# A build-time planner that knows TensorE's tile widths, matmuls over rows of zeros, and copies for whichever engine is free

## The chip, the cores and the metric

The kernel runs on one core of a Trainium2 chip. The metric is the device time of one execution in microseconds (us), the median of several runs. Profiles are of one execution each; their span, from the first to the last instruction, is some 50 us shorter than the device time.

## The reference

16 images of 336x336 pixels become 441 tokens each, 128 text tokens follow, so there are 16 sequences of T = 569 tokens of D = 256. Two layers work on them, all in f32:

```
h = concat(tokens(x), txt)
# layer 0
h = h + window_attention(layernorm(h))      # windows of 64, 8 heads, shifted
h = h + experts(layernorm(h))               # 8 experts, the 2 best of each token
# layer 1
h = h + phasor_attention(layernorm(h))
h = h + lstm_block(layernorm(h))

def phasor_attention(x):                    # a linear attention with a running state
    key_phase   = tanh(gelu(x @ Wk1 + bk1) @ Wk2 + bk2) * freq * pi
    query_phase = tanh(gelu(x @ Wq1 + bq1) @ Wq2 + bq2) * freq * pi
    V = x @ Wv + bv
    memory = cumsum(exp(i key_phase) * V, over tokens)
    r = real(sum(memory * exp(-i query_phase))) / sqrt(position * 64)
    return x + (layernorm(r) * ln_w + ln_b) @ Wo + bo

def lstm_block(x):                          # 569 steps, one after another
    gates = x @ W_ih.T + b + h @ W_hh.T     # i, f, g, o
    c = sigmoid(f) * c + sigmoid(i) * tanh(g);  h = sigmoid(o) * tanh(c)
    # then a sum over earlier and later tokens with a gate from h @ W_lin
```

## The kernel before

All work is cut into small generators. Each `yield` names an engine and a planned duration (`yield "ACT", 0.58`), and the instructions that follow it are that piece of work. A planner, `Order` (its `run`), holds many such streams at once. It keeps the time at which each engine is planned to be free, always takes the piece that can start first (ties go to the lower rank, then to the earlier stream), and emits its instructions. All of this happens when the program is built: on the chip, each engine executes a fixed list in that order, and only semaphores hold it back.

`first = Order()` plans the first part: `features` and `projections` (image features), `tokens` (attention of the tokenizer, two streams), `norms`, `windows` (window attention, four streams), `routing`. `plan = Order()` plans the rest: `experts`, and then the flow. Engines are TensorE (PE), VectorE (DVE), ScalarE (ACT) and GpSimd (POOL); a `+` after a name (`DVE+`) stands for the use of a resource that DVE and POOL share.

In the flow, four background streams work on units of two pairs of sequences and one column chunk of 128 rows: `fronts` (two slots, function `front`: combining the experts' outputs, norm, keys, queries and values) and `backs` (two slots, function `back`: reading from the state, norm, output projection, norm, and the LSTM's input projection, split into three bf16 pieces by L1495, L1497, `rest_of_pieces`, and written to XPD). `add_to_state` (ds, L1348) adds each chunk to the running state S. A batch is four units of one chunk, and two batches make one block of 64 time steps for the LSTM; `stats` and `norm` are shared helpers.

The stream `steps()` is the LSTM chain. It is special: its operations have a fixed table of planned durations (`STEP`), and the planner takes background pieces only into the gaps that its function `limits` leaves. The rule is this line, with `spare` the overrun that is allowed:

```
spare = 0.15 if engine == "PE" else 0.0 if "+" in engine else 0.1
...
if start + taken > end + spare and not (start > s.ready + 8.0 and start < end - 0.5):
    continue
```

One LSTM step is 16 hidden matmuls 16 columns wide (L1614, planned as `hidden`), then the next step's two `input` matmuls (L1584, L1585), gates on ACT (L1628, L1631), products and cell on DVE (L1634, L1640), two 32x32 transposes (L1646, L1649), tanh (L1652), and X, the new hidden state (L1654). `all_sums` handles the sums after every 16 steps.

PE's array can be used in narrower tiles. Matmuls with 64 output columns go side by side (tokens L548, L576; windows L681, L696, L736; state reads L1431), 32 wide ones in the router (L781) and in `hidden`; ds takes 64 rows of keys at a time, and the biases of V and of the output projection are added by matmuls of three rows (three bf16 pieces of the bias, times ones: L1283, L1451). The planner before adds one constant, `SWITCH = 0.09`, whenever a piece marked `"small"` follows one that is not, or the reverse.

Of the kernel before, what the change touches and what calls it, by code (L numbers as in the profile page):

```python
# [17 lines left out]
D = 256  # L18
# [85 lines left out]

ENGINES = {
# [5 lines left out]

HOP = 0.06
OVERLAP = {"PE": 0.0, "DVE": 0.08, "ACT": 0.1, "POOL": 0.03}
DRAIN = 0.17
SWITCH = 0.09
# [26 lines left out]
class Order:  # L142
    def __init__(self):
        self.free = dict.fromkeys(("PE", "DVE", "ACT", "POOL", "+"), 0.0)
        self.events, self.ends = {}, dict.fromkeys(STEP, 0.0)
        self.now, self.table, self.small = 0.0, None, False
        self.forks, self.held, self.freed = [], set(), {}
# [63 lines left out]
    def run(self, streams, until=None):  # L211
        streams = [s if isinstance(s, Stream) else Stream(s) for s in streams]
        for s in streams:
            if s.head is None and not s.over:
                self.advance(s)
        while self.forks or not all(s.over for s in (until or streams)):
            for s in self.forks:
                self.advance(s)
            streams = [s for s in streams if not s.over] + self.forks
            self.forks = []  # L220
            for s in streams:
                self.settle(s)
            if all(s.over for s in (until or streams)):
                continue
            chain = [s for s in streams if s.chain and not self.blocked(s)]
            limit, best = {}, None
            if chain:
                limit = self.limits(chain[0])
                engine, us = STEP[chain[0].head][:2]
                best = (limit[uses(engine)[0]], -1, -1, chain[0], engine, us)  # L230
            for n, s in enumerate(streams):
                if s.chain or self.blocked(s):
                    continue
                engine, us = s.head[:2]
                kind = s.head[2] if len(s.head) > 2 else None
                if engine == "PE":
                    us += SWITCH * ((kind == "small") != self.small)
                elif kind not in (None, self.table):
                    us += 1.3
                start = max([s.ready] + [self.free[e] for e in uses(engine)])  # L240
                end = min(limit.get(e, 1e9) for e in uses(engine))
                spare = 0.15 if engine == "PE" else 0.0 if "+" in engine else 0.1
                taken = us - OVERLAP[engine.strip("+")]
                if start + taken > end + spare and not (start > s.ready + 8.0 and start < end - 0.5):
                    continue
                if best is None or (start, s.rank, n) < best[:3]:
                    best = (start, s.rank, n, s, engine, us)
            assert best is not None, "all streams wait"
            start, _, _, s, engine, us = best
            if s.chain:  # L250
                for e in uses(engine):
                    self.free[e] = start + us
                self.ends[s.head] = start + STEP[s.head][2]
                s.ready = start + us
                if engine == "PE":
                    self.small = s.head == "hidden"
            else:
                for e in uses(engine):
                    self.free[e] = start + (us if e == "+" else us - OVERLAP[e])
                if engine == "PE":  # L260
                    self.small = len(s.head) > 2
                elif len(s.head) > 2:
                    self.table = s.head[2]
                s.ready = start + us
            was = engine
            self.advance(s)
            if not s.chain and not s.over and s.head[0].strip("+") != was.strip("+"):
                s.ready += HOP + DRAIN * (was == "PE")


@with_exitstack
def kernel(ctx: ExitStack, tc: tile.TileContext, a: dict, out: bass.AP):
# [264 lines left out]
    def tokens(slot):  # L537

        last = NIMG - 384
        for n in range(slot, 7 * NP, 2):  # L540
# [4 lines left out]
            for m in range(2):  # L545
                yield "PE", 0.8, "small"
                for s in range(2):
                    nc.tensor.matmul(  # L548
                        sc[64 * s : 64 * s + 64, :NIMG], QT[s][:, m, 64 * c : 64 * c + 64],
                        fTs[2 * p + s][:, m, :], start=(m == 0), stop=(m == 1),  # L550
                    )
# [20 lines left out]
            for t in range(4):  # L572
                m = min(128, NIMG - 128 * t)
                yield "PE", 0.5, "small"
# [66 lines left out]
    def windows(slot):  # L641

        kb, vb = KB[slot], VB[slot]
        for n in range(slot, NC * NP, WINDOWS):
# [33 lines left out]
            for m in range(2):  # L678
                yield "PE", 0.46, "small"
# [12 lines left out]
            for w in range(2):  # L692
                for k in range(2):
                    yield "PE", 0.26, "small"
# [36 lines left out]
            for m in range(2):  # L731
                for w in range(2):
                    yield "PE", 0.16, "small"
# [22 lines left out]
    def routing():  # L756

        for p, lo, hi in PARTS:
            u, n = f"{p}_{lo}", hi - lo
            pr = wk.tile([128, n, E], F32, name=f"pr{u}", tag="pr", bufs=1)  # L760
            for g0 in range(lo, hi, 4):
# [16 lines left out]
                for k in range(2):  # L778
                    yield "PE", 0.42, "small"
# [172 lines left out]
    one3 = ls.tile([3, 128], BF16, name="one3")  # L952
    nc.vector.memset(one3, 1.0)

    bias3 = {n: ls.tile([3, 2, D], BF16, name=f"{n}3") for n in ("l1_bv", "l1_bo")}
# [217 lines left out]


# [27 lines left out]
    def norm(src, mv, rstd, name, slot):  # L1202
        xn = wk.tile([128, 2, D], F32, name=name, tag=f"xn{slot}")
        for c in range(src.shape[1]):
            yield ("DVE", 0.54) if name[0] == "r" else ("DVE+", 0.42)
            nc.vector.tensor_scalar(
                xn[:, c, :], src[:, c, :], mv[:, c, 0:1], rstd[:, c : c + 1],
                ALU.subtract, ALU.mult,
            )
        return xn  # L1210
# [12 lines left out]
    def front(p, c, n, at, slot):  # L1223
# [34 lines left out]
        yield "ACT", 0.55  # L1258
        nc.scalar.copy(xT, tr)
# [22 lines left out]
        yield "PE", 0.32  # L1282
# [8 lines left out]
        yield "ACT", 0.58  # L1291
        nc.scalar.copy(V[:, both, :], v)
        z = bank(f"z{u}", slot).rearrange("p (k n) -> p k n", k=2)
        y = wk.tile([128, 2, 256], F32, name=f"fy{u}", tag=f"fy{slot}")
# [37 lines left out]

    def add_to_state(p, c, u, slot, S2, kT, V, at):

        for s in range(2):
            half = slice(64 * s, 64 * s + 64)
# [6 lines left out]
            for j in range(2):  # L1343
                yield ("PE", 0.43) if c == 8 else ("PE", 0.53, "small")
                lhs, rhs = (
                    (kT[:, j, :], own[:, j, :]) if c == 8 else (kT[half, j, :], V[half, at + j, :])
                )
                nc.tensor.matmul(ds[:, j, :], lhs, rhs, start=True, stop=True)  # L1348
# [31 lines left out]
    def back(p, c, batch, at, slot, late=False):  # L1380
# [24 lines left out]
        if not late:  # L1405
# [3 lines left out]
            kT = wk.tile([128, 2, 128], F32, name=f"kT{u}", tag=f"kT{slot}")  # L1409
            yield "ACT", 0.38  # L1410
            nc.scalar.copy(kT, sc[:, :, 1, :])
# [12 lines left out]
        for j in range(2):  # L1424
            yield "PE", 256 * COLUMN
            nc.tensor.matmul(r[:, j, :], w[:, j, :], V[:, at + j, :], start=True, stop=not reads)
            if reads:
                yield "PE", 0.55, "small"
# [11 lines left out]
        for k in range(2):  # L1440
            yield "DVE", 0.34 if c8 else 0.54
            src, to = tr[:, k, :], nT[:, k, :]
            if c8:
                src = src.rearrange("p (b x) -> p b x", x=64)[:, :, r0 : r0 + 32]
                to = to.rearrange("p (b x) -> p b x", x=32)
            nc.vector.tensor_scalar(
                to, src, col("ln_w", k), col("ln_b", k), ALU.mult, ALU.add
            )
        po = bank(f"po{u}", slot)[:, : D * n].rearrange("p (k n) -> p k n", k=n)
        yield "PE", 0.32 if n == 2 else 0.2  # L1450
# [25 lines left out]
        yield "ACT", 0.3 * n  # L1476
        nc.scalar.copy(xT, tr)  # L1477
        to = XPD[block].rearrange("(i q b) t d -> i q b t d", i=3, q=4)
        for i in range(2 * n):
# [14 lines left out]
            yield "ACT", 0.58  # L1494
            nc.scalar.copy(pieces[:, 0, :], mm)  # L1495
# [248 lines left out]
    with tc.manual_schedule(engines=ENGINES):  # L1744
# [5 lines left out]
        wk = bg.enter_context(tc.tile_pool(name="pha", bufs=1))  # L1750
        chain, rest = Stream(steps(), True), Stream(all_sums())
# [165 lines left out]
```

## Time and profile before

| | before |
|---|---|
| time, median of 3 | 3776.37 us (3773.66 to 3778.86) |
| span of the profiled execution | 3726.4 us, mean granted clock of PE 0.965 |
| busy: PE, DVE, ACT, POOL | 87%, 57%, 38%, 25% |
| hidden matmuls, L1614 | 9088 records, the costliest group, 612.8 us |
| chain that ended last | PE 33%, DVE 12%, ACT 5% of the span |

The page divides the span into 40 slices of 93 us, and the digits there are busy tenths. A group's line gives the source line, the engine, the operation, the tile written and the tiles read, the shape, the count, busy time and mean duration, and at its end how long the engine had been idle ahead of it and what ended that idle time. In a line of stretches, each engine has its busy time and its number of instructions (x), then follow the clock that PE was granted, and the share and rate of the DMA. A matmul in f32 appears as two records of one instruction each, which start apart by their streaming time and overlap in duration, so starts tell more than durations.

### The profile page before, as it was taken

What the parts mean: (1) busy time and instruction counts of PE and PEld (TensorE: products, weight loads), DVE (VectorE), ACT (ScalarE), POOL (GpSimd) and SP (SyncE); (2) the same over time, 40 slices, a digit from 0 to 9 for tenths busy, and PEclk for the clock granted to TensorE, in tenths of its full rate; (3) what the DMA queues carried; (4) which work ended last, traced back from release to release, by engine and by line L of the source; (5) the groups of instructions that cost most, each with busy time, mean ns of one, the idle gap of its engine ahead of it and who ended that gap; (6) DMA issues with size and microseconds to landing.
All of it is one profiled execution on the core that took longest, in us unless ns stands there. A gap on an engine that the chain in (4) does not pass through costs nothing.

```text
span 3726.4 us, 67881 instructions
## 1 busy us (share of the span) xinstructions
PE 3249.1 (87%) x24854; PEld 2095.9 (56%) x24854; DVE 2121.5 (57%) x6447; ACT 1398.8 (38%) x4098; POOL 944.0 (25%) x1627
## 2 busy tenths in 40 slices
PE   6989998899839999996899999999999999998663
PEld 3656565555538888885556555555555555544331
DVE  4666666665631111113476677777777777676444
ACT  3444454444312222223444444444444444333220
POOL 1244344443520000004433322222222222121000
PEclk9999999999969999998999999999999999999997
DMA  4111112100166666653324333333333333333214
GB/s 159 53 57 61 62 67 75 41 28 22 46 216 221 228 231 225 231 175 101 98 79 120 104 84 94 99 91 97 97 94 103 100 87 91 91 106 117 86 38 101
DMA packets 276950, 398.13 MB, mean 107 GB/s; under 512 B 29008, under 2 KB 234056, under 8 KB 263560
## 3 DMA queue, kind: packets, MB, share of 16 engines
q1 hardware_dynamic: 254712, 347.44, 29.9%
q0 software_dynamic: 13824, 37.77, 3.4%
q10 hardware_dynamic: 8080, 8.57, 0.7%
q8 instruction: 196, 3.21, 0.4%
q14 instruction: 138, 1.13, 0.1%
HBM read 256.60 MB, written 136.97 MB: 106 GB/s over the span
## 4 chain that ended last, share of the span: by engine, by line
PE 33%; DVE 12%; ACT 5%; issue 2%; POOL 1%; DMA 1%; SPq 0%; ACTq 0%; DVEq 0%; POOLq 0%
PE g L1614 13%; PE xm_False L1486 4%; DVE ab L1634 2%; PE g L1584 2%; PE v L1287 2%; DVE act L1640 2%; ACT th L1652 2%; DVE cT L1646 2%; ACT act L1628 2%; PE z L1298 2%; PE eq L1267 2%; PE ek L1267 2%; DVE X L1654 1%; PE ds_False L1348 1%; PE po_False L1455 1%
## 5 line engine op out<-in xcount | busy, mean ns | idle before, releaser
L1614 PE MATMUL g<-W_hh,X 128*16 128x256 f32 x9088 | 612.8, 388 | 169.6 <-DVE X L1654 165.6
L1614 PEld LDWEIGHTS g<-W_hh,X 128*16 128x16 f32 x9088 | 208.9, 96 | 464.0 <-DVE X L1654 332.9
L1628 ACT ACTIVATE act<-g 128x192 f32<-128x192 f32 x568 | 187.9, 331 | 593.8 <-PE g L1614 592.2
L1634 DVE SCALAR_TENSOR_TENSOR ab<-act 128x128 f32<-128x128 f32 x568 | 172.2, 303 | 388.0 <-ACT act L1628 380.9
L1239 POOL DMA_INDIRECT yg<-YS,yat x144 | 142.9, 992 | 660.1 <-DMA YS<-ys 622.8
L1153 ACT ACTIVATE hT<-hp,w 128x256 f32<-128x256 f32 x316 | 132.5, 472 | 456.2 <-PE hp L1146 293.3
L1160 PE MATMUL y<-w,hT 128*128 128x256 f32 x1264 | 289.9, 382 | 6.3 <-ACT hT L1153 2.5
L1364 POOL TENSOR_TENSOR xp_False<-left_False,xp_False 128x256 bf16<-128x256 f32 x272 | 182.4, 691 | 425.9 <-ACT xp_False L1361 408.5
L1146 PE MATMUL hp<-xt,w 128*128 128x256 f32 x1264 | 285.8, 379 | 0.0
L1486 PE MATMUL xm_False<-W_ih,dxT_False 128*128 128x256 f32 x1088 | 272.4, 384 | 9.0 <-ACT dxT_False L1477 7.5
L1652 ACT ACTIVATE th<-cT 128x32 f32<-128x32 f32 x569 | 130.0, 228 | 359.9 <-DVE cT L1646 353.9
L1160 PEld LDWEIGHTS y<-w,hT 128*128 128x128 f32 x1264 | 236.7, 190 | 46.8 <-ACT hT L1153 16.1
L1166 DVE TENSOR_TENSOR ys<-y,w 128x512 f32<-128x512 f32 x79 | 54.6, 691 | 357.8 <-PE y L1160 357.8
L1146 PEld LDWEIGHTS hp<-xt,w 128*128 128x128 f32 x1264 | 239.0, 190 | 33.9
L1486 PEld LDWEIGHTS xm_False<-W_ih,dxT_False 128*128 128x128 f32 x1088 | 196.4, 191 | 39.7 <-ACT dxT_False L1477 10.5
L1654 DVE SCALAR_TENSOR_TENSOR X<-toT,th 128x32 f32<-128x32 f32 x569 | 116.3, 204 | 116.9 <-ACT th L1652 116.8
L1584 PEld LDWEIGHTS <-pick 128*128 128x128 bf16 x569 | 54.6, 96 | 214.5 <-issue 212.1
L663 PE MATMUL wqk<-wxT,wqkv 128*128 128x128 f32 x1152 | 164.2, 285 | 10.7 <-ACT wxT L657 10.5
L663 PEld LDWEIGHTS wqk<-wxT,wqkv 128*128 128x128 f32 x1152 | 144.6, 193 | 41.4 <-ACT wxT L657 19.9
L872 POOL DMA_INDIRECT XS<-XN,at x144 | 149.3, 1037 | 58.8 <-DVE at L865 29.4
L1584 PE MATMUL g<-xp,pick 128*128 128x256 bf16 x569 | 161.4, 284 | 1.8 <-DMA xp<-XPD 1.8
L1585 PE MATMUL g<-xp,pick 76*128 76x256 bf16 x569 | 157.9, 278 | 3.6 <-DMA xp<-XPD 3.6
(337 smaller groups left out, 6416.7 us busy)
## 6 DMA issues: line engine op xcount, KB each, us to landing
w<-in_wpack SPq DMA_DIRECT2D x79, 1154.0 KB
XPD<-xp_False SPq DMA_DIRECT2D x408, 128.0 KB
xp<-XPD SPq DMA_DIRECT2D x71, 512.0 KB
taps<-in_taps SPq DMA_DIRECT2D x16, 1764.0 KB
xs<-XS SPq DMA_DIRECT2D x79, 256.0 KB
YS<-ys SPq DMA_DIRECT2D x79, 256.0 KB
xp<-XPD SPq DMA_DIRECT2D x71, 256.0 KB
HD<-h SPq DMA_DIRECT2D x72, 128.0 KB
```

The lines of the kernel that those rows point to most:

```text
L663: nc.tensor.matmul(qk[:, j, m, :], wqkv[:, k, D * j + 128 * m : D * j + 128 * m + 128], xT[:, k, :], start=(k == 0), stop=(k == 1),)
L1146: nc.tensor.matmul(hp[:, i, :], w1[:, k, hc * 128 : (hc + 1) * 128], xT[:, k, :], start=(k == 0), stop=(k == 1),)
L1160: nc.tensor.matmul(y[:, i, :], hT[:, hc, 128 * i : 128 * i + 128], w2[:, hc, :], start=(hc == 0), stop=(hc == 3),)
L1364: nc.gpsimd.tensor_tensor(pieces[:, 2, h], left[:, h], pieces[:, 1, h], ALU.subtract)
L1486: nc.tensor.matmul(mm[:, 256 * part : 256 * part + 256], xT[:, k, j * 128 : (j + 1) * 128], Wih[:, k, at_ : at_ + 256], start=(k == 0), st ...
L1584: nc.tensor.matmul(g, pick[:, 0, :], xp[:, 0, t, :], start=True, stop=False)
L1585: nc.tensor.matmul(g, pick[:76, 1, :], xp[:76, 1, t, :], start=False, stop=(k, t) == (0, 0))
L1614: nc.tensor.matmul(g[32 * q : 32 * q + NB, :D], before[:, kk, :], Whh[:, kk, q * D : (q + 1) * D], start=False, stop=(kk == 1),)
L1628: nc.scalar.activation(act[:, :192], g[:, :192], AF.Tanh, scale=0.5)
L1634: nc.vector.scalar_tensor_tensor(ab, act[:, :128].rearrange("p (g x) -> p g x", g=2), 1.0, act[:, 128:].rearrange("p (g x) -> p g x", g=2) ...
L1652: nc.scalar.activation(th, cT[:, :, :NB], AF.Tanh, scale=0.5)
L1654: nc.vector.scalar_tensor_tensor(X[:, :, t, :], toT[:, :, :NB], 1.0, th, ALU.add, ALU.mult)
```

## The change

The change has four parts.

The planner's costs. `SWITCH` is replaced by costs to enter and to leave a tile width (`TO_TILES`, `FROM_TILES`), per width, and pieces are marked "64" or "32" instead of "small", with new durations. A piece of another width than PE has now is ranked as if it started 0.3 us (`SAME_TILES`) later. The overrun into the chain's gaps falls from 0.15 to 0.1 for PE and from 0.1 to 0 for DVE and ACT.

Free choice. A piece can be `"DVE/ACT"` with one duration for each; the planner takes the engine where it starts first, and the helper `copy` emits the instruction for that engine. Copies of fxT, V, dxT, kT, the first bf16 piece, and the scale-and-shift operations of the norm of r and of nT are such pieces. For this the norm of r is computed as scale and bias, which needs one small operation (`less`).

Full tiles. The bias matmuls run over 128 rows, of which all but three are zero in the bias. For ds, the keys of the two halves lie in two persistent tiles for each slot, each with zeros in the other half's rows, and the matmul takes all 128 rows of V.

Memory. `fy` shares the buffers of `xn`, as the persistent key tiles need room.

```diff
-SWITCH = 0.09
+TO_TILES = {None: 0.0, "32": 0.11, "64": 0.15}
+FROM_TILES = {None: 0.0, "32": 0.1, "64": 0.19}
+SAME_TILES = 0.3
...
-                if engine == "PE":
-                    us += SWITCH * ((kind == "small") != self.small)
...
-                spare = 0.15 if engine == "PE" else 0.0 if "+" in engine else 0.1
...
+                either = s.head[0] == "DVE/ACT"
+                kind = s.head[2] if len(s.head) > 2 and not either else None
+                for engine, us in zip(("DVE", "ACT"), s.head[1:]) if either else [s.head[:2]]:
+                    other = kind != self.tiles if engine == "PE" else kind not in (None, self.table)
+                    if other:
+                        us += 1.3 if engine != "PE" else FROM_TILES[self.tiles] + TO_TILES[kind]
+                    start = max([s.ready] + [self.free[e] for e in uses(engine)])
+                    key = start + (SAME_TILES if other and engine == "PE" else 0.0)
...
+                    spare = 0.1 if engine == "PE" else 0.0
...
-                yield "PE", 0.8, "small"
+                yield "PE", 0.76, "64"
...
-    one3 = ls.tile([3, 128], BF16, name="one3")
+    one3 = ls.tile([128, 128], BF16, name="one3")
...
-    bias3 = {n: ls.tile([3, 2, D], BF16, name=f"{n}3") for n in ("l1_bv", "l1_bo")}
+    bias3 = {n: ls.tile([128, 2, D], BF16, name=f"{n}3") for n in ("l1_bv", "l1_bo")}
...
+    def copy(to, src, scale=None, bias=None):
+        if plan.chosen == "DVE":
...
+        if name[0] == "r":
+            less = wk.tile([128, 2], F32, name=name + "_less", tag=f"less{slot}", bufs=1)
+            yield "DVE", 0.17
+            nc.vector.scalar_tensor_tensor(
+                less, mv[:, :, 0], -1.0, rstd, ALU.mult, ALU.mult
+            )
+            for c in range(src.shape[1]):
+                yield "DVE/ACT", 0.54, 0.46
+                copy(xn[:, c, :], src[:, c, :], rstd[:, c : c + 1], less[:, c : c + 1])
+            return xn
...
-        yield "PE", 0.32
+        yield "PE", 0.22
         nc.tensor.matmul(v, one3, bias3["l1_bv"], start=True, stop=False)
...
-        yield "ACT", 0.58
-        nc.scalar.copy(V[:, both, :], v)
+        yield "DVE/ACT", 0.69, 0.58
+        copy(V[:, both, :], v)
...
-                yield ("PE", 0.43) if c == 8 else ("PE", 0.53, "small")
-                lhs, rhs = (
-                    (kT[:, j, :], own[:, j, :]) if c == 8 else (kT[half, j, :], V[half, at + j, :])
-                )
-                nc.tensor.matmul(ds[:, j, :], lhs, rhs, start=True, stop=True)
+                yield "PE", 256 * COLUMN
+                rhs = own[:, j, :] if c == 8 else V[:, at + j, :]
+                nc.tensor.matmul(
+                    ds[:, j, :], kT[0 if c == 8 else s][:, j, :], rhs, start=True, stop=True
+                )
...
-            kT = wk.tile([128, 2, 128], F32, name=f"kT{u}", tag=f"kT{slot}")
-            yield "ACT", 0.38
-            nc.scalar.copy(kT, sc[:, :, 1, :])
+            kT = keys_of[slot]
...
+            for s in range(0 if c8 else 2):
+                half, other = (slice(64 * i, 64 * i + 64) for i in (s, 1 - s))
...
+                yield "DVE/ACT", 0.41, 0.38
+                copy(kT[s][half], sc[half, :, 1, :])
...
-            yield "ACT", 0.58
-            nc.scalar.copy(pieces[:, 0, :], mm)
+            yield "DVE/ACT", 0.69, 0.58
+            copy(pieces[:, 0, :], mm)
```

## The prediction

> **What bounds the kernel now.** I read the page first for the stages, then busy time by stretch, then the chain's own lines, then TensorE (PE) in order of time.
>
> ```profile
> PE   6989998899839999996899999999999999998663
> PEclk9999999999969999998999999999999999999997
> ```
>
> Four stages stand here: the first part (0 to 1040 us), the experts (1090 to 1700), the flow with the LSTM chain (1705 to about 3430), and the chain alone. The clock hardly ever dips, so it explains none of them.
>
> ```profile
> core 0: us, PE busy (x) PEld busy (x) DVE busy (x) ACT busy (x) POOL busy (x), PEclk, DMA share, GB/s
> 50.00:950.00 900.00, 818.64 (x6632) 522.63 (x6630) 586.55 (x1499) 415.55 (x1111) 358.93 (x631) 0.99 0.15 54
> 1705.00:1984.00 279.00, 245.61 (x1470) 169.62 (x1470) 156.66 (x459) 127.67 (x305) 122.66 (x190) 0.95 0.35 99
> 2000.00:3300.00 1300.00, 1212.18 (x10490) 681.68 (x10489) 943.28 (x3217) 570.10 (x1825) 341.06 (x582) 0.98 0.34 94
> ```
>
> PE is busy 91%, 88% and 93% of these stretches; no other engine passes 73%. ACT is at 44% in the flow where DVE is at 73%. Then the LSTM's last line, L1654 (one X per step), in the same kind of view:
>
> ```profile
> 2000.00:3300.00 1300.00, 84.82 (x411) 0.98 0.34 94
> 3430.00:3680.00 250.00, 15.72 (x82) 0.99 0.19 65
> ```
>
> A step takes 1300/411 = 3.16 us beside background work and 250/82 = 3.05 us over the whole last stretch; from X to X its typical value there is 2.92 and its mean 2.94. So the chain is the clock of the flow, and the background costs each step 0.22 us. From hop to hop (mean of the crowded steps less that of the free ones) 0.11 us of it is hidden matmuls that wait for PE, 0.03 slower hidden matmuls, 0.02 and 0.03 waits for DVE and ACT, and the rest DVE operations stretched beside GpSimd. The background is just fast enough: a block of 64 steps is written 64 steps after the last one, at steps 149, 213, 277, 341, 405, some ten steps before it is needed. Only block 1 is late: it is complete at 1984 us, while the chain has stood since 1930.
>
> Last, the price of a change of tile width, in PE's timeline:
>
> ```profile
> 402.81 0.38 PE L653 MATMUL wtr<-ident,wxn 128*128 128x128 f32 x2
> 403.13 0.45 PE L736 MATMUL wav<-wPT,VB 128*64 128x64 f32 x8
> ...
> 405.37 0.44 PE L696 MATMUL wv<-wqkv,wxT 128*64 128x128 f32 x4
> 405.74 0.49 PE L663 MATMUL wqk<-wxT,wqkv 128*128 128x128 f32 x2
> ...
> 2372.33 0.27 PE L1585 MATMUL g<-xp,pick 76*128 76x256 bf16 x1
> 2372.54 0.39 PE L1283 MATMUL v<-l_bv,one 3*128 3x512 bf16 x1
> 2372.86 1.56 PE L1287 MATMUL v<-Wv,fxT 128*128 128x256 f32 x6
> ```
>
> Starts of single records: a 128x128 transpose is followed by the next after 0.109 us, but by a 64-wide one after 0.203; the first 64-wide pair then takes 0.100 where the others take 0.058: 0.14 to go in. Going out, 0.202 instead of 0.109 and then 0.214 instead of 0.110: 0.19. A round trip costs 0.33 us. The bias matmul with three rows pays the same way: 0.21 instead of 0.11 ahead of it, 0.32 instead of 0.216 for its 512 columns, and 0.1 more on the next matmul, about 0.3 us.
>
> **What the Trainium skill says.** "TensorEngine Tiling (Array Packing)", Key Properties: a change of tiling mode, not of tile alone, drains TensorE. The trace agrees, with 0.14 in and 0.19 out. "ScalarE: Activation LUTs", What ACT_TABLE_LOAD costs: 186 ns plus 0.833 ns an element, and about 93 ns more for each operand that is a pointer to one value a partition. For 256 elements with scale and bias both pointers this gives 585 ns; the trace has 595 for hb (L1324), the same form. "SBUF — State Buffer", SBUF: two separate sides: the port pair of DVE and GpSimd is an exclusive lock. The trace agrees (the ab of 0.28 us takes 0.60 at 2434.93, beside the two GpSimd subtractions that start at 2434.71); the change leaves this alone.
>
> **The change part by part.**
>
> First part. Nothing here but the plan's costs and its new liking for the tile width that PE has. Walking PE's matmuls from 50 to 1040 us by shape, I count 306 entries into narrower tiles from full ones; 72 windows with three narrow groups each (scores, values, output), 56 token units with two, and 24 router groups would make 352 at most, so the old order merges only 13%. 306 x 0.33 = 101 us of PE. How many could merge? Lining up each narrow group with the operation that made its input gives a wait of about 1.1 us, so 352 x 1.1 / 950 = 0.41 narrow groups lie ready at any time, and 0.37 a microsecond x 0.3 us = 0.11 more come ready inside the 0.3 us that the plan now accepts. At least one is there with a chance of 1 - exp(-0.52) = 0.4. Merging 40% leaves 352 x 0.6 = 211 entries, 95 fewer: 95 x 0.33 = 31 us. PE is busy 91% and its waits do not shrink, so I count three quarters: 24 us. Bounds: 10 (idle waits of up to 0.3 us eat most) to 40.
>
> Experts: full tiles only and no chain to respect; no change, 0 us.
>
> Bias matmuls: 36 for v (L1283) and 32 for po (L1451), 0.3 us each: 20 us of PE gone. State keys: 64 pairs ds (L1348, 64 rows) each pay 0.09 in, 0.10 inside, and up to 0.2 out, which is free when the hidden matmuls, waiting for X anyway, come next: 0.2 to 0.4, I take 0.3, 19 us. Together 39 us of about 1600 us of flow. What it costs: two copies of 64 partitions instead of one of 128 (373 ns, L1411), some 0.4 us more for each of 32 units, and one tiny DVE operation (0.17 us) for 36; 19 us over two engines with 27% and 56% free, beside PE: nothing on the path. The memsets of zero rows are few and lie beside PE too.
>
> Where these 39 us count. Before block 1 the chain waits for the background: about 10 of the bias matmuls and 9 of the pairs lie before 1984, 19 x 0.3 = 6 us, and 2 more from copies going to the free engine: 8 us. Afterwards the chain sets the pace, and PE time saved only lets the background end sooner. In a block of 64 steps PE gives it 64 x 1.58 = 101 us; 8 bias matmuls and 8 pairs save 4.8 us, three steps. Over seven blocks some 22 steps become free ones, 22 x 0.22 = 5 us.
>
> The crowded step. Hidden matmuls find PE taken 44 us in total over 411 steps. Steps filled with four full matmuls (1.73 us into a gap of 1.70) stay allowed, as the overrun is 0.03 and the new limit 0.1; those cost 0.1 each and remain. What goes is what the plan priced too low: bursts that end in bias, state or score matmuls account for about 24 us, and half of it, 12, should go. DVE operations that run into ab cost about 13 us, and the limit of 0 for DVE and ACT instead of 0.1 should take 7 off. That makes 19, or 20 us over 450 crowded steps. The other side: DVE gets less room, since statistics of 0.41 no longer go in between toT and X. Per step the background wants 943/411 less 1.2 us of chain, about 1.1 us, and the large gap between X and ab is 1.55 us: it fits, with the normalisations able to leave for ACT. There one with two pointers takes 0.59 where the plan says 0.46 (L1324), so an ACT operation may end 0.13 late; with some 80 such moves and a third of them in a tight place, 80 x 0.13 / 3 = 3 us back, which I leave inside the rounding.
>
> Sum: 24 + 8 + 5 + 20 = 57 us. 3776 - 57 = 3719.
>
> **The rivals.**
> - Only the first part gains (3752). The tighter limits cost the background as much room as the cheaper matmuls give, steps stay at 3.16. For it: DVE at 73% and spare cut to 0. Against: DVE's gap is larger than its need. 3776 - 24.
> - More merges (3675). Once narrow groups wait for each other they pile up: 40 in the first part, 10 before block 1, 6 from the earlier end, 45 if half of the crowded step's 0.22 us goes. For it: PE starts half of the groups late, so there is a queue. Against: dependencies alternate narrow and full in each stream.
> - Slower (3804). The background needs 68 steps a block: 4 x 7 = 28, less the ten in hand, 18 steps of 3.1 us = 56 us of starving, while waits for an equal width eat the gain of the first part; 56 - 28 from the other two places, net 28 more. For it: the background is only just fast enough today. Against: it gets 4.8 us a block lighter.
> - Nothing measurable (3776): the sizes cancel.
>
> **How the numbers follow.** Forecast 0.5, only the first part 0.18, more merges 0.12, slower 0.13, nothing 0.07. Faster is 0.5 + 0.18 + 0.12 = 0.80. The range runs from 3675, the third case, to 3785: it leaves out the slower case (0.13) and the deeper half of the merges (0.06).
>
> **What would show it.** Right: entries into narrow tiles between 50 and 1040 us fall from 306 to about 210, and the experts begin some 24 us sooner; ds and bias matmuls at full width with the 0.1 us steps gone; block 1 complete about 30 us earlier in absolute time; a crowded step of about 3.12 us; ACT above 44% and DVE under 73% in the flow. Wrong: the first part as long as before with more idle PE; blocks written only when the chain already stands, as gaps over 4 us between X and X near steps 96, 160, 224; or waits of th for ACT that grow by the long normalisations.

## The result and the profile after

The changed kernel takes 3628.09 us (median of 4 runs, 3622.94 to 3640.28) where the kernel before takes 3777.49 in the same comparison: a ratio of 0.9611, with an interval of 0.9584 to 0.9637. That is 149 us, where 57 were forecast, and 47 us below the low end of the range.

```profile
PE   6999999899399999978888999889999899988662
PEclk9999999999699999989999999999999999999997
```

These are the page's 40 slices after the change. The first dent, the wait between first part and experts, has moved from slice 12 to slice 11 of a shorter span. The rest looks alike, so stretches have to be measured.

The kernel before takes 3728 to 3733 us on some chips (the faster chips in what follows) and 3776 to 3786 us on others (the slower chips), so two traces are compared only when they come from one chip, or from chips of one sort where that is said. The profile shown ahead of the prediction came from a faster chip, while the 3776 us beside it were measured on slower ones: the profiled execution itself took 3728.33 us, 2 us more than its span of 3726.4. The some 50 us between span and device time that are spoken of there are this difference between chips. The next two groups of lines are the kernel before and the changed kernel, both profiled on one slower chip: PE, PEld, DVE, ACT and POOL busy in the first part and over the LSTM's steps 64 to 448, and then the X of those steps alone.

```profile
50.00:1040.00 990.00, 885.46 (x7120) 567.50 (x7118) 633.86 (x1620) 445.19 (x1190) 394.44 (x691) 0.97 0.15 52
2128.00:3369.00 1241.00, 1137.82 (x9797) 637.99 (x9795) 883.81 (x3006) 529.20 (x1703) 318.21 (x540) 0.97 0.33 93
...
2128.00:3369.00 1241.00, 79.04 (x385) 0.97 0.33 93
```

```profile
50.00:944.00 894.00, 818.36 (x7121) 568.88 (x7123) 619.88 (x1613) 439.29 (x1189) 394.54 (x686) 0.99 0.16 57
2019.00:3206.00 1187.00, 1076.44 (x9788) 631.90 (x9801) 869.89 (x2981) 557.72 (x1777) 316.54 (x540) 1.00 0.34 96
...
2019.00:3206.00 1187.00, 74.87 (x385) 1.00 0.34 96
```

The number of matmuls in the first part is the same within one (x7120, x7121), and they are done in 894 us instead of 990. PE is busy 67 us less and idle 29 us less (104.5 to 75.6). In the flow the same 384 steps take 1187 us instead of 1241, PE is busy 61 us less, its clock rises from 0.97 to 1.00, and ACT is busy 28 us more, DVE 14 less. The spans are 3787.6 and 3631.7 us, and they differ by stage like this (the last column is the first profile of before against a profile of the changed kernel on another faster chip; the last digit depends on where a stage is cut):

| stage | forecast, us | same slower chip | faster chips |
|---|---|---|---|
| first part, up to the experts' first transpose | -24 | -96 | -82 |
| experts | 0 | -3 | +1 |
| combining, block 1, up to step 64 | -8 | -11 | -12 |
| steps 64 to 448 | -20 | -54 | -47 |
| the rest, with the earlier end of the background | -5 | +8 | +10 |
| sum | -57 | -156 | -130 |

Two terms of the sum are far off, the first part and the crowded step (a step of the LSTM chain with background work beside it, here steps 64 to 448).

Where a step's time goes, hop by hop, is worked out from the starts and ends of its instructions in the trace (ns, mean of steps 64 to 448; "X to hid" is the wait for PE, "hid" the 16 hidden matmuls, "ab to cell" holds the product ab, "cT to th" the wait for ACT's tanh):

| | X to hid | hid | hid to act | act to ab | ab to cell | cell to cT | cT to th | th to X | X | sum, us |
|---|---|---|---|---|---|---|---|---|---|---|
| before, slower chip | 143 | 1097 | 143 | 385 | 342 | 281 | 370 | 264 | 206 | 3.231 |
| changed, slower chip | 114 | 1057 | 125 | 404 | 325 | 263 | 345 | 263 | 195 | 3.090 |
| before, faster chip | 159 | 1089 | 68 | 396 | 341 | 281 | 365 | 263 | 206 | 3.167 |
| changed, faster chip | 126 | 1057 | 71 | 403 | 324 | 262 | 346 | 262 | 194 | 3.046 |

The gain of 0.14 and 0.12 us lies in five places at once: waits for PE, faster hidden matmuls, DVE's two middle hops, tanh, X. A step alone takes 2.94 us before and after.

### The profile page after: what moved, and what is told of

Read it like the earlier page. It is cut to its first block, busy times and chain, and to the rows that moved or that the text cites. A ratio compares the mean times of both kernels' runs of the same rounds, so it can differ in the third digit from the quotient of the medians.

```text
span 3623.0 us, 68059 instructions
## 1 busy us (share of the span) xinstructions
PE 3129.6 (86%) x24854; PEld 2105.2 (58%) x24854; DVE 2113.3 (58%) x6450; ACT 1419.1 (39%) x4173; POOL 953.9 (26%) x1627
## 4 chain that ended last, share of the span: by engine, by line
PE 30%; DVE 15%; ACT 5%; issue 3%; POOL 1%; DMA 1%; ACTq 0%; SPq 0%; another core or an unknown queue 0%; DVEq 0%; POOLq 0%
PE g L1656 13%; PE xm_False L1528 4%; DVE ab L1676 2%; DVE cT L1688 2%; ACT th L1694 2%; ACT act L1670 2%; DVE act L1682 2%; DVE X L1696 2%; PE g L1626 1%; PE eq L1299 1%; PE ek L1299 1%; DVE y L1750 1%; DVE y L1745 1%; PE po_False L1497 1%; PE v L1319 1%
## 5 line engine op out<-in xcount | busy, mean ns | idle before, releaser
L1656 PE MATMUL g<-W_hh,X 128*16 128x256 f32 x9088 | 604.3, 384 | 206.6 <-DVE X L1696 188.9
L670 PE MATMUL wqk<-wxT,wqkv 128*128 128x128 f32 x1152 | 152.3, 281 | 6.0 <-ACT wxT L664 5.7
```

What stands on the lines that cost most here:

```text
L670: nc.tensor.matmul(qk[:, j, m, :], wqkv[:, k, D * j + 128 * m : D * j + 128 * m + 128], xT[:, k, :], start=(k == 0), stop=(k == 1),)
L1656: nc.tensor.matmul(g[32 * q : 32 * q + NB, :D], before[:, kk, :], Whh[:, kk, q * D : (q + 1) * D], start=False, stop=(kk == 1),)
```

## The experiments

**The pair on one chip.** Nothing is edited in either.

> The kernel before, unchanged, for its profile beside the others of this set. In the set with e1 the same flow ran with dips of PE's clock to half in every half block and crowded steps of 3.25 us, where the first profile had 3.16. Theory: what the profile of before didn't show of the gain (149 us by time, 103 by spans) is such dips, so here the crowded step is 3.2 to 3.25 us with a dip about every 100 us and the span about 3780. Rival: the extra lies outside the flow, and the crowded step is 3.16 again.

> The changed kernel, unchanged, in the same set. Theory: its order leaves no step of the crowded stretch without work on PE, the clock doesn't dip there, crowded step 3.09 to 3.11, time 3625 to 3640. Rival: with this set's chip its flow dips as e3's and e4's did, and the time is 3660 or more.

Measured: 0.9597 (0.9569 to 0.9625) for the changed kernel; their traces gave the tables above.

**The first part alone.** The kernel before gets the changed planner, with its prices and durations, for the first part only (`Tiled` is the changed `Order`); `plan` stays as it was. A second kernel takes the liking out of that planner.

```diff
-    first = Order()
+    first = Tiled()
```

```diff
-SAME_TILES = 0.3
+SAME_TILES = 0.0
```

> The kernel before, with the changed planner, its prices and durations in the first part alone; the flow keeps its old planner. If the first part's gain is independent of the flow, the experts start where they start in the changed kernel: first transpose of the experts at about 1003 us instead of 1084, and the span falls by about 80 us to 3645. Rival: part of the 81 us comes from something else that the change does (it touches nothing else before the experts), then the start is later than 1020 us.

> As e1, with SAME_TILES = 0: the same prices and durations, but no ranking of other widths 0.3 us later. Theory of merged widths: entries into narrow tiles go back to about 300 and the gain of the first part falls to under 20 us (span about 3710). Rival, truer prices: the plan's better knowledge of how long PE is taken gives an order with fewer waits by itself, and at least 40 of the 80 us stay (span below 3690).

Measured: 3692.75 us with the liking, 0.9742 (0.9712 to 0.9771), and 3789.55 us without, 1.0011 (1.0 to 1.0021). The experts begin at 1010 us and at 1109; before has 1106. Both in the view of stretches, first with the liking, then without:

```profile
50.00:944.00 894.00, 817.87 (x7138) 569.69 (x7136) 619.93 (x1613) 439.94 (x1190) 394.62 (x686) 0.99 0.16 58
```

```profile
50.00:1043.00 993.00, 886.55 (x7124) 568.74 (x7122) 636.16 (x1619) 444.83 (x1189) 399.41 (x698) 0.97 0.15 53
```

So the gain of the first part hangs on the ranking (the liking for the width that PE has). The prices, which only tell the planner when PE will be free, do nothing by themselves; the ranking without the new prices was not tried. Entries from full into narrower tiles, counted by walking PE's matmuls: 306 before, 314 without the liking, 139 with it. PE in order of time shows what it does (changed kernel):

```profile
410.12 0.27 PE L570 MATMUL tpt<-ident,tP 128*57 128x128 f32 x1
410.33 0.64 PE L788 MATMUL lg<-rxT,gw 128*32 128x128 f32 x16
410.90 1.08 PE L688 MATMUL wsc<-KB,wq 128*64 128x256 f32 x8
411.82 0.40 PE L743 MATMUL wav<-wPT,VB 128*64 128x64 f32 x8
```

Three narrow groups of three different streams, the router's and two windows', follow each other with no full-width work between them. The planner of before takes each as it comes ready, as the lines ahead show, where a narrow group follows full-width work, and full-width work a narrow group, within 3 us.

167 entries fewer at the 0.33 us of the prediction are 55 us of the 67 that PE is less busy; stretches in which PE is granted half its clock fall from 44 us to 14 in the first part (the wait at its end left out), which is worth up to 15 us more. That PE also idles 29 us less was in no reckoning. It follows from the edit of the ranking too, but how was not tried.

**Each part of the flow alone.** The kernel before with the full-width biases and keys (with the memory and the planned durations that go with them, but the old planner and no free choice), and the kernel before with the tighter limits and nothing else.

```diff
-    bias3 = {n: ls.tile([3, 2, D], BF16, name=f"{n}3") for n in ("l1_bv", "l1_bo")}
+    bias3 = {n: ls.tile([128, 2, D], BF16, name=f"{n}3") for n in ("l1_bv", "l1_bo")}
...
-                yield ("PE", 0.43) if c == 8 else ("PE", 0.53, "small")
+                yield "PE", 256 * COLUMN
```

```diff
-                spare = 0.15 if engine == "PE" else 0.0 if "+" in engine else 0.1
+                spare = 0.1 if engine == "PE" else 0.0
```

> The kernel before with full-width bias and key matmuls alone (old planner, copies on ACT). Theory: the pace is the chain's, so it wins 10 to 20 us at most against 3786. Rival: the lighter bursts also free the chain of waits for PE and it wins over 30 us.

> The kernel before with the tighter overrun alone (0.1 for PE, 0 for DVE and ACT). By e3 the overrun was worth 0.12 us in each crowded step of the changed kernel. Theory of tight limits: the step falls by 0.05 us or more here too and the time by 20 to 45 us. Rival: without full tiles and free choice the background no longer keeps up, blocks need more than 64 steps, the chain starves at their borders, and nothing is won or time is lost.

Measured: 0.9987 (0.9978 to 0.9997) and 1.0006 (0.9997 to 1.0015); crowded steps 3.144 and 3.139 us on a faster chip, where before has 3.167. Neither alone gives anything that counts. The free choice alone, and the flow with the new prices and ranking alone, were not run.

**Each part taken away from the changed kernel.** The overruns of before; the engine of before for every free choice (one of seven such lines is shown); biases over three rows and keys over 64 rows again, with prices for both.

```diff
-                    spare = 0.1 if engine == "PE" else 0.0
+                    spare = 0.15 if engine == "PE" else 0.0 if "+" in engine else 0.1
```

```diff
-            yield "DVE/ACT", 0.69, 0.58
+            yield "ACT", 0.58
```

```diff
-        yield "PE", 0.22
+        yield "PE", 0.22, "32"
...
-                yield "PE", 256 * COLUMN
+                yield ("PE", 256 * COLUMN) if c == 8 else ("PE", 256 * COLUMN, "64")
```

> The changed kernel with the old overrun into the chain's gaps (0.15 for PE, 0.1 for DVE and ACT). Theory of the prediction: the tighter limits took about 20 us out of the crowded steps, so this one has steps of 3.14 us or more instead of 3.11 and a span 10 to 20 us longer (3633 to 3643). Rival: the shorter steps come from the full-width matmuls and the prices, then within 5 us of 3623.

> The changed kernel with every free choice fixed to the engine of before (copies on ACT, the scale-and-shift pieces on DVE). Theory: with DVE's gaps closed at 0 overrun, the choice is what keeps the background fast; without it blocks take over 64 steps and the span grows by 10 to 30 us. Rival: the choice is worth nothing or costs (ACT pieces with two pointers take 0.55 where 0.46 is planned, gates wait for ACT 48 times in the crowded stretch): span within 5 us of 3623 or shorter.

> The changed kernel with the bias matmuls back to three rows and the state keys back to one copy and 64 rows, priced as narrow pieces (32 and 64). Theory of the prediction: 39 us of PE come back, of which only those before block 1 and the end of the background count, so 13 us slower than the changed kernel (about 3650). Rival: the background becomes slower than 64 steps a block under the tight limits, the chain starves, and it loses 40 us or more.

| | ratio to before | crowded step, us | before's, same sort of chip |
|---|---|---|---|
| old overruns | 0.9748 (0.9719 to 0.9776) | 3.211 | 3.231 |
| no choice | 0.9726 (0.9694 to 0.9758) | 3.195 | 3.231 |
| narrow again | 0.9793 (0.9776 to 0.981) | 3.151 | 3.167 |

The first two ran on one slower chip, on which the flow of before, in the two runs of the first part alone, takes 3.25 and 3.24 us a step; the changed kernel has 3.090 on a slower chip and 3.046 on a faster one. Whichever part goes, most of the gain of the flow goes with it. Three parts can't each be worth most of it. Either they need each other, or something else is lost each time.

**Truer durations.** The changed kernel with measured durations in the plan: 0.56 instead of 0.46 for ACT's scale-and-shift with two pointers, 0.59 for hb, and longer sums on DVE.

```diff
-                yield "DVE/ACT", 0.54, 0.46
+                yield "DVE/ACT", 0.54, 0.56
...
-            yield "ACT", 0.45
+            yield "ACT", 0.59
```

> The changed kernel with the durations that the profile shows for the sums on DVE (0.64, 0.75, 0.66 for 16 steps instead of 0.40, 0.66, 0.40) and for ACT pieces with two pointers (0.56 and 0.59 instead of 0.46 and 0.45). Theory: waits for DVE ahead of ab (0.04 us a step) and some of the waits for ACT go, crowded step 3.04 to 3.07, 10 to 20 us faster than the changed kernel. Rival: the dearer pieces find no gap, the background needs more than 64 steps a block and the gain is lost.

Measured: 0.9743 (0.9721 to 0.9764), crowded step 3.171 us. The wait that the longer ACT pieces cause did go (act to ab 368 ns instead of 403), but waits for PE rose from 126 to 225 ns. A plan with better numbers made a worse order.

**The clock.** PE at half clock fills 72 us of steps 64 to 448 before and none after, on the same slower chip. To see what that is worth by itself, matmuls that nobody reads fill PE's idle steps, in the kernel before and in the changed one.

```diff
+                if plan.idle > 0.8 and before is not None and j < len(BLOCKS) - 2:
...
+                    nc.tensor.matmul(gates[nxt][:, :D], ident, Whh[:, 0, :D], start=True, stop=True)
```

> The kernel before, order unchanged, with one matmul that nobody reads (ident times W_hh, 128x256, about 0.43 us) ahead of the hidden matmuls of each of the 59 steps in which the plan leaves PE idle for over 0.8 us. Theory of the clock: the dips in the crowded stretch vanish though PE has more to do, the crowded step falls to 3.12 or less and the time falls by 30 to 50 us to about 3735. Rival: the dips are a mere sign, the extra matmuls cost or do nothing: time within 8 us of before.

> The changed kernel with the same filler matmuls in its 87 idle steps. Theory: the changed kernel has no dips in the crowded stretch, so nothing is to be won: within 8 us of the changed kernel. Rival: on this chip it dips too, then it gains 10 to 40 us.

Measured: before with fillers 0.9966 (0.995 to 0.9982), 14 us at half clock left, crowded step 3.210 us; changed with fillers 0.9585 (0.9568 to 0.9603), where the changed kernel has 0.9597. The time falls by 13 us, less than half of what was expected, and the step by 0.02 us, which is 8 of the 54 us; the fillers take time on PE themselves, so the clock may be worth somewhat more. In the changed kernel nothing that can be measured is left to win from it.

**The limits, or the order that comes out of them.** Three very small edits of the changed kernel, and itself again: PE's overrun at 0.08, at 0.15 (DVE and ACT left at 0), and the flow's liking at 0.25.

```diff
-                    spare = 0.1 if engine == "PE" else 0.0
+                    spare = 0.08 if engine == "PE" else 0.0
```

```diff
-                    spare = 0.1 if engine == "PE" else 0.0
+                    spare = 0.15 if engine == "PE" else 0.0
```

```diff
-    plan = Order()
+    plan = Order(0.25)
```

> The changed kernel without any edit, as the reference of this set. On one chip of the earlier sets the kernel before took 3729 us, on others 3785 us. If the change's gain does not depend on the chip: a ratio of 0.957 to 0.964 to the kernel before of the same set, and a crowded step (steps 64 to 448) of 3.09 us where before has 3.23, or 3.03 to 3.09 where before has 3.17. If part of the gain is a cure for what only the slower chips show (stretches of half clock, late gates): on the faster chip a ratio of 0.967 to 0.972.

> The changed kernel with the overrun allowed for PE at 0.08 us instead of 0.1. By the limits alone nothing should be lost: a tighter limit lets less background run into the chain, so the crowded step is 3.08 to 3.11 us, 0.99 to 1.005 of the changed kernel's time in this set. If the flow's gain hangs on the particular order that the planner happens to find, in which the same few steps repeat from block to block, a change of 0.02 us in one limit is enough to lose it: crowded step 3.14 to 3.22 us, stretches of half clock come back (30 to 70 us of them in steps 64 to 448), and the time rises by 20 to 50 us.

> The changed kernel with the overrun for PE back at the 0.15 us of before, the one for DVE and ACT left at 0. It splits the earlier run in which all the old overruns came back (crowded step 3.211 us, 48 us slower). If PE's overrun did that: crowded step 3.19 to 3.22 us here too. If the overrun of DVE and ACT did it: 3.08 to 3.12 us here. If any other order than the changed kernel's does it: 3.14 to 3.22 us, with the loss spread over waits that have nothing to do with PE (ab to cell, cell to its transpose, the transpose to tanh).

> The changed kernel with the liking for the tile width that PE has at 0.25 us instead of 0.3 in the plan of experts and flow; the first part is planned as before with 0.3. The emitted order differs in some ninety lines of PE only. If the parts of the change as such make the flow's gain: crowded step within 0.02 us of the changed kernel's, time within 8 us. If the particular order does: the step moves by 0.03 to 0.12 us, where the order departs, and the time by 10 to 45 us.

| | time, us | ratio to before | crowded step | half clock, us |
|---|---|---|---|---|
| changed | 3595.41 | 0.9629 (0.9606 to 0.9653) | 3.046 | 0 |
| overrun 0.08 | 3643.20 | 0.9749 (0.9722 to 0.9775) | 3.127 | 48 |
| overrun 0.15 | 3642.41 | 0.976 (0.9739 to 0.9781) | 3.116 | 24 |
| liking 0.25 | 3604.45 | 0.965 (0.9628 to 0.9671) | 3.045 | 0 |

A limit tighter by 0.02 us costs 48 us, and one looser by 0.05 costs 47. So the tightness of PE's limit is not what wins. The two are not two independent tries, though: in 81% of steps 64 to 448 they run the same other PE instructions, and th and ab (see below) are late at the same steps in both. They count as one other order, reached from both sides. With the liking at 0.25, every engine's list in the trace is, line by line, that of the changed kernel (the trace doesn't tell buffers of one name apart, and the ninety lines of the expectation don't show in it), and the step is the same to 0.001 us; the run says nothing about other orders, only how well a given order repeats its time (here to 9 us).

What the orders differ in can be named. Compared with the changed kernel, overrun 0.08 loses 0.081 us a step, 31 us in 384 steps. About 11 us of this are hidden matmuls at half clock, 7 a gelu ahead of th, 4 casts of pieces ahead of th, 7 ab held up beside GpSimd, and 4 a longer X; other hops give 2 back. Some 8 to 12 us more are lost ahead of step 64. This is ACT in order of time, first in the kernel before (on the slower chip), then with overrun 0.08:

```profile
2393.26 0.22 ACT L1631 ACTIVATE to<-g 128x64 f32<-128x64 f32 x1
2393.49 1.28 ACT L1273 ACT_TABLE_LOAD   x1
2394.79 0.47 ACT L1273 ACTIVATE gk<-ek,cols 128x256 f32<-128x256 f32 x1
2395.16 0.22 ACT L1652 ACTIVATE th<-cT 128x32 f32<-128x32 f32 x1
```

```profile
2478.85 0.22 ACT L1673 ACTIVATE to<-g 128x64 f32<-128x64 f32 x1
2479.09 1.28 ACT L1305 ACT_TABLE_LOAD   x1
2480.38 0.47 ACT L1305 ACTIVATE gk<-ek,cols 128x256 f32<-128x256 f32 x1
2480.76 0.22 ACT L1694 ACTIVATE th<-cT 128x32 f32<-128x32 f32 x1
```

and the same pieces in the changed kernel:

```profile
2167.11 0.62 ACT L1395 CAST xp_False<-left_False 128x512 bf16<-128x512 f32 x1
2167.62 0.37 ACT L1191 COPY kT<-sc_False 64x256 f32<-64x256 f32 x1
2168.07 0.23 ACT L1694 ACTIVATE th<-cT 128x32 f32<-128x32 f32 x1
2168.32 1.28 ACT L1305 ACT_TABLE_LOAD   x1
2169.61 0.47 ACT L1305 ACTIVATE gk<-ek,cols 128x256 f32<-128x256 f32 x1
2169.98 0.32 ACT L1670 ACTIVATE act<-g 128x192 f32<-128x192 f32 x1
```

In the first two, table load and gelu (gk) go between `to` and th, and th starts 1.18 us after its input's transpose starts, instead of 0.34. In the third they fill the gap between th and the next act exactly. The place repeats: with overrun 0.08, th is late behind gk at steps 151, 183, 215, 247, 279, 311, 343, 375, 407, every 32; before had it ten times, at 82, 146, 178 and so on to 402; the changed kernel has it at step 82 and then never again. With overrun 0.08, ab takes over 0.4 us in 21 steps (before 24, changed kernel 1), among them every 32 steps from 141 to 397, and each time GpSimd's subtraction for the third piece runs. DVE and GpSimd in order of time, with overrun 0.08:

```profile
2447.39 0.76 DVE L1238 TENSOR_SCALAR fxn<-fh,f_mv,f_rstd 128x256 f32<-128x256 f32 x1
2448.07 0.75 DVE L1676 SCALAR_TENSOR_TENSOR ab<-act 128x128 f32<-128x128 f32 x1
2448.86 0.23 DVE L1682 SCALAR_TENSOR_TENSOR act<-ab 128x64 f32<-128x64 f32 x1
```

```profile
2446.42 0.94 POOL L1218 TENSOR_TENSOR f_rstd<-f_rstd,mhalf 128x2 f32<-128x2 f32 x1
2447.34 1.34 POOL L1398 TENSOR_TENSOR xp_False<-left_False,xp_False 128x256 bf16<-128x256 f32 x2
```

ab takes 0.75 us beside the pair of subtractions, 0.29 otherwise. By the page of the Trainium skill cited ahead of the result ("SBUF — State Buffer", SBUF: two separate sides) the later of two such instructions waits for the whole of the earlier. The trace fits in that ab ends only after the pair does, at 2448.82 and 2448.68 us.

32 steps are one batch of four units, and two batches make a block. In the changed kernel 96% of steps 90 to 384 run the same other PE instructions as the step 32 later; with overrun 0.08 it is 75%, before 83%. So these orders are patterns of 32 steps, and what they contain is paid about ten times. Not every order is such a pattern. With narrow again it is 65%, and with old overruns, no choice, full tiles alone, tight alone and true durations only 2 to 12%, and their late spots lie mostly scattered. Nor is the pattern as such good or bad: before, changed and overrun 0.08 all have one.

Six variants on faster chips (narrow again, full tiles alone, tight alone, true durations, overruns 0.08 and 0.15) give crowded steps of 3.116 to 3.171 us, mean 3.141, where before has 3.167. The changed kernel's 3.046 lies 0.07 below the best of them. No variant was measurably better than it.

## Why the prediction was wrong

**What held.** PE bounds the first part, and the chain paces the flow. ds and the biases at full width run as forecast: a record of ds takes 382 ns in the mean instead of 417, and the matmul behind a bias starts 0.22 us after it where it was 0.32 (PE in order of time, changed kernel):

```profile
2395.27 0.38 PE L1315 MATMUL v<-l_bv,one 128*128 128x512 bf16 x1
2395.49 1.03 PE L1319 MATMUL v<-Wv,fxT 128*128 128x256 f32 x4
```

Up to the first step of block 1 the gain was 7 to 13 us where 8 were counted. This may be luck: that step comes 280 to 285 us after the flow's first transpose in the changed kernel, 291 to 293 before, but 294 with overrun 0.08, which has all the parts. ACT rose to 47% of steps 64 to 448 (557.72 of 1187). DVE is at 73%, where under 73 was expected (71% before, on the same chip). The experts did not change. The direction was right.

**The step that failed first: "Merging 40% leaves 352 x 0.6 = 211 entries", and then "I count three quarters: 24 us".** Measured: 139 entries, so that 61% of the 352 groups are merged, and 96 us (82 between faster chips). The model took the 0.41 narrow groups that lie ready on average in the old order and asked how often another comes within 0.3 us. But by its code the ranking works both ways: while PE is narrow, full-width work is ranked later as well, so that groups can pile up and go together, and the old order's average is no measure of the new one. The lower count is measured; that it comes about by this piling up is read from the code and the lines above. The rival "more merges" said just this and put 40 us on it, too little still. And the three quarters, taken because idle time was expected to eat a part, had the wrong sign: idle time fell by 29 us. The unit price of 0.33 us stands: 167 x 0.33 = 55 of 67 us of busy time, the rest is within what the clock can give.

**The second: "That makes 19, or 20 us over 450 crowded steps", a step of 3.12.** Measured: 54 us, 3.090 from 3.231 on the slower chip, and 47 us, 3.046 from 3.167, on faster ones. The prediction took half of one cause and half of another, and put the others at nothing. Of ab's delays beside GpSimd it said "the change leaves this alone"; they fell from 24 to 1. th's waits behind gelu, which it left as they were, fell from ten (fourteen on the slower chip) to one. Of the clock it said that it "hardly ever dips"; half clock in these steps fell from 58 us (in the very profile that it read) and 72 us (slower chip) to 0, and the hidden matmuls became 32 to 40 ns faster, 12 to 15 us in 384 steps. The prediction treated late spots as a cloud of chance collisions that a rule thins out. In the kernel before and in the changed one they are a pattern of 32 steps, so that a bad spot comes about ten times or hardly at all; in tight alone, which has no pattern, the long ab's are thinned from 24 to 7 and the step still takes 3.139 us. That overruns of 0.08 and 0.15 give 3.127 and 3.116 us, near the 3.12 that was forecast, doesn't confirm the reckoning: at 0.15 PE's limit isn't tightened at all. That the change as written would find 3.046 could not be read from the profile of before; it would have been an honest reason for a range that reaches 50 us lower.

**The base of the sum.** The prediction took its time from slower chips and its steps from a faster one. That is not what made it fail: the gain is 138 us on a faster chip (0.9629) and 149 us on slower ones (0.9611 and 0.9597).

**The third, small: "some 22 steps become free ones, 22 x 0.22 = 5 us".** The background doesn't finish sooner. It completes blocks at steps 90, 154, 218, 282, 346, 410, exactly 64 apart, and its last matmul (xm) comes at step 495 where before has 486; the last stage is 8 to 10 us longer. Perhaps the tighter limits gave the time on PE back as room; that was not tried.

**The doubt about two-pointer pieces on ACT** was right in kind: they take 0.55 to 0.56 us where the plan has 0.46, and act to ab grew by 7 to 19 ns. An estimate by the sum in the Trainium skill's "ScalarE: Activation LUTs", What ACT_TABLE_LOAD costs, is 0.585 us for 256 elements. The pieces measured here, which read PSUM, lie a little below it (0.553 and 0.556), hb, which reads SBUF, a little above (0.595). Pricing them truly didn't pay: the order became another one.

**What stays open.** Why the planner finds a good order with 0.1 and not with 0.08 or 0.15 isn't explained. That the order decides, and not the tightness of PE's limit, is shown by the step times; that a given spot causes its share is read from the hops and not tried one by one. Small edits around the free choice and the full tiles were not made, so it is not shown whether the good order needs these parts or is merely lost with any edit. The ranking and the prices were never taken out of the flow alone. Nor is it settled why PE idles less in the first part.

## What to carry to other kernels

A greedy planner's order can jump with a constant: 0.02 us in one limit moved the time by 48 us. Where the order repeats (here every 32 steps), each late spot is paid many times, so look for spots that come back at a fixed distance, make a few neighbouring plans, see that they really are different orders, and don't credit the constant that was last turned. Where engines pay for changing modes, rank ready work by the mode the engine is in; telling the planner the price without changing the ranking gained nothing (1.0011 against 0.9742). An estimate of how much work can be merged must ask what the new rule makes pile up, not only what lies ready under the old one.

## What the runs showed of the hardware

The kernel before differs by 1.5% between chips, the changed kernel by about 1%. On slower chips the gates start late after the hidden matmuls at fixed steps. This is ACT, kernel before, on such a chip:

```profile
2446.11 0.33 ACT L1628 ACTIVATE act<-g 128x192 f32<-128x192 f32 x1 [2.99 <-PE po_False L1455]
```

It comes 1.7 us after the last hidden matmul, at steps 162, 194, 226 and so on to 386; on a faster chip no act of the kernel before is more than 0.5 us late in steps 64 to 448. Over these steps act starts 0.125 to 0.149 us after the hidden matmuls in all profiles from slower chips, and 0.068 to 0.075 in all from faster ones. In the changed kernel on the slower chip such spots are there too, but of 0.5 to 1.1 us. The cause isn't settled.

On the slower chip half clock follows such spots. The same stretch of the kernel before, with the hidden matmuls alone:

```profile
2440.00:2451.00 11.00, 3.21 (x52) 1.14 (x56) 0.97 0.21 58
2451.00:2457.60 6.60, 3.77 (x32) 0.93 (x32) 0.53 0.22 66
2457.60:2464.00 6.40, 2.12 (x32) 0.73 (x32) 1.00 0.54 166
```

32 hidden records take 3.77 us of PE in the middle line and 2.12 in the last. PE had waited 2.26 and 1.67 us just before, with 1.4 us of work between. By the Trainium skill's "TensorE: Matmul & The Clock Gate", Part 1, the clock falls to half after an idle window of about 3.4 us. The stretches seen are 3.4, 6.8 and 10.2 us long, which agrees with such a window, but no single wait ahead of this one was as long as that. From step 163 they come every 32 steps as well. Late gates are not needed for them: on the faster chip the kernel before has 58 us at half clock in steps 64 to 448, with no wait of PE over 1.7 us in the 8 us ahead of a stretch.
